# Edge counts as logarithms in the scores of graph layer 1, and softmax sums from a column of ones in its products

## The chip, the cores and the metric

The kernel runs on one core of a Trainium2 chip. The metric is the time of one execution on the device in microseconds (us). A profiled execution is looked at beside it: its span is the time from the first to the last instruction that the profiler saw.

## What is computed

Four graph networks work one after the other on 512 nodes with 768 features each, over 8704 edges; after each there is a residual addition and a normalisation. Layer 0 is a graph attention with eight heads, layer 1 a relational graph attention, layer 2 three relational convolutions, layer 3 two convolutions. The change is in layer 1, which has three edge types and is computed twice: with four heads of 192 features, then with one head of 768. One such convolution is:

```python
xr = jnp.einsum('nd,rdf->rnf', x, W)
oi, oj = xr[etype, dst], xr[etype, src]
alpha = leaky_relu(oi @ q + oj @ k, 0.2)
m = segment_max(alpha, dst)
e = exp(alpha - m[dst])
z = segment_sum(e, dst)
a = e / (z[dst] + 1e-16)
out = segment_sum(a * oj, dst)     # by heads; then the bias
```

Edges are not walked one by one. The kernel has counted how many edges of type r go from node n to node d, and keeps these counts c[d, r, n]. Then out[d] is the sum over (r, n) of c * exp(alpha - m) * xr[r, n], divided by the sum over (r, n) of c * exp(alpha - m).

## The kernel before, in words

Nodes lie in NB = 4 blocks of 128 partitions, and the three types side by side in the free dimension, so a score tile `z` has 128 x 1536 elements. All weights are used in a split form: `split_piece` (L735) loads a third of a 768 x 384 half of a matrix (`raw`, SP's queue), makes three parts of it (L753 on ScalarE, L754 and L755 on VectorE), and stays one half ahead of its use. `product` (L785) multiplies with these parts; between its first twelve and its last six matmuls of a block ScalarE scales the PSUM bank (L802).

**The counts.** `decode3` (L1168) runs four times inside the products of layer 0's heads 2 and 3: it takes three 3-bit digits out of a packed integer (L1175), ScalarE casts each to bf16 (L1176), SP stores 384 KB (`c3_store`), and VectorE sums and checks the counts (L1179 to L1184).

**Layer 1, first convolution.** Three types times two halves of `product` fill `xr[r]`; `columns` and `keys` make the two halves of the scores. Then `run` (L1374) goes through 16 steps s = (block b, head h). Its order is written out by hand: `soft` of step s+2, then the transposes (`turn`) of step s+1, then the sum of step s; Tile then orders each engine's instructions by its own priorities. A step is:
- `soft` (L1349): ScalarE makes z = key + column in three instructions (L1352). `softmax` (L833) takes the leaky maximum (L837, VectorE), negates, adds the mask and takes the minimum in one instruction (L839), takes the exponential (L843, ScalarE), multiplies by the counts while summing (L845, VectorE) and takes the reciprocal (L849).
- `turn` (L1357): twelve 128 x 128 transposes of z on TensorE (L1363), and three copies from PSUM (L1366), which `evacuate` gives to ScalarE and VectorE in turn (L84, L86).
- `sum1` (L1406): twelve matmuls of 192 columns (L1415; each fp32 matmul is two instructions in the profile), then one VectorE instruction that multiplies by the reciprocal and adds the bias (L1419). With a block's last head comes an ELU (L1424 to L1426), and a step later its transposes and split (L767 to L777).

`load_cm` (L1341) loads a block's counts, 384 KB in bf16, into one of two buffers, and makes the mask from them (L1346). z and the transposed weights have two buffers each.

**Layer 1, second convolution.** `product` fills `xr` again; as each block is complete, two dot products of 768 elements on VectorE (`dots`, L1440) give the scores' columns. The last ones gate the keys (L1450 to L1453), since these overwrite the rows that `dots` reads. Then `run` goes through four steps with 24 matmuls of 384 columns (L1473) in each.

Of the kernel before, what the change touches and what calls it, by code (L numbers as in the profile page):

```python
# [8 lines left out]
F32 = mybir.dt.float32  # L9
# [16 lines left out]
SOFT_EPS = 1e-16  # L26
LN_EPS = 1e-5
# [6 lines left out]
def gnn_stack_kernel(ctx: ExitStack, tc: tile.TileContext, a: dict, out: bass.AP):  # L34
# [73 lines left out]
    nc.vector.memset(eps, LN_EPS)  # L108
    ones = const.tile([P, 1], F32, tag="ones", name="ones")
# [46 lines left out]
    c3_store = dram.tile([NB, P, R3 * N], BF16, tag="c3", name="c3_store")  # L156
# [549 lines left out]
    def split_layers():  # L706
# [161 lines left out]
        with (  # L868
# [299 lines left out]
            def decode3(b):  # L1168

                v = work.tile([P, N], I32, tag="elu_y", name=f"packed_{b}")  # L1170
                nc.sync.dma_start(v, packed_store[b])
                c3 = g.tile([P, R3, N], BF16, tag="c3", name=f"c3_{b}")
                for r in range(R3):
                    d = work.tile([P, N], I32, tag="elu_e", name=f"d3_{b}_{r}")
                    digit(d, v, r)  # L1175
                    nc.scalar.copy(c3[:, r, :], d)  # L1176
                nc.sync.dma_start(c3_store[b], c3.rearrange("p r n -> p (r n)"))
                t = work.tile([P, N], F32, tag="elu_e", name=f"total_{b}")
                nc.vector.tensor_add(t, c3[:, 0, :], c3[:, 1, :])  # L1179
                nc.vector.tensor_tensor_reduce(  # L1180
                    out=t, in0=t, in1=c3[:, 2, :], scale=1.0, scalar=0.0,
                    op0=ALU.add, op1=ALU.add, accum_out=seen[:, 0, b : b + 1],
                )
                nc.vector.tensor_reduce(seen[:, 1, b : b + 1], t, axis=AX.X, op=ALU.max)  # L1184
# [88 lines left out]
        with (  # L1273
# [3 lines left out]
            xr = [rp.tile([P, NB, D], F32, tag=f"xr{r}", name=f"xr{r}") for r in range(R3)]  # L1277
# [9 lines left out]
            def columns(r, b):  # L1287

                rT = wide(f"r1_rT{r}_{b}")
                for j in range(2):  # L1290
                    pt = bank(f"r1_t{r}_{b}_{j}")
                    for i in range(HK):
                        c = j * HK + i
                        nc.tensor.transpose(
                            pt[:, i * P : (i + 1) * P], xr[r][:, b, c * P : (c + 1) * P], ident
                        )
# [26 lines left out]
            def project(left, r, j, name, also=None):  # L1323
                def keep(b, po):
                    evacuate(xr[r][:, b, columns_of(j)], po[:, :HD])
# [15 lines left out]
            def load_cm(b, name):  # L1341

                cnt = work.tile([P, R3 * N], BF16, tag="cnt", name=f"{name}_cnt{b}")
                nc.sync.dma_start(cnt, c3_store[b])
                mask = rp.tile([P, R3 * N], BF16, tag="mask", name=f"{name}_mask{b}")
                nc.vector.tensor_scalar(mask, cnt, 0.0, NEG, op0=ALU.is_equal, op1=ALU.mult)  # L1346
                return cnt, mask

            def soft(cm, key, bias, name):  # L1349
# [404 lines left out]
```

## Time and profile before

| | us |
|---|---|
| median of three runs | 1746.12 (1742.83 to 1746.43) |
| the profiled execution | 1745.2 |
| its span | 1743.3 |
| busy in the span: TensorE (PE) | 1614.6, 93% |
| VectorE (DVE) | 1219.2, 70% |
| ScalarE (ACT) | 755.7, 43% |
| layer 1's first run of 16 steps, from the first sum's first matmul to the last sum's end | 828.6 to 946.9 |

Times in rows are microseconds, those marked "mean ns" nanoseconds. PE is a matmul, PEld the load of its weights, SPq an issue of a transfer on SP's queue. A group's row gives the line, engine, operation, output and inputs with shapes, how often, then busy time and mean duration, then the idle time of the engine just before such instructions and what ended it. PEclk is the granted TensorE clock, 1.00 being full. One execution's 1.9 us outside its span are no part of the rows.

### The profile page before, as it was taken

How to read it: one execution, taken by the hardware profiler on the slowest of the kernel's cores; microseconds unless marked ns; L12 is line 12 of the kernel's file. 1: busy time of each engine (PE TensorE's matmuls, PEld its weight loads, DVE VectorE, ACT ScalarE, POOL GpSimd, SP SyncE). 2: the span in 40 equal slices, each digit the busy share in tenths (PEclk: the TensorE clock that was granted, in tenths of full speed). 3: DMA queues.
4: the chain of work that ended last, by engine and by line, in shares of the span. 5: the costliest groups of instructions: out<-in, count | busy, mean ns of one | idle time of the engine just before them, and what ended most of it. 6: DMA issues, size and time to landing. Idle time of an engine off the chain costs nothing.

```text
span 1743.3 us, 22110 instructions
## 1 busy us (share of the span) xinstructions
PE 1614.6 (93%) x8527; PEld 1446.1 (83%) x8527; DVE 1219.2 (70%) x2177; ACT 755.7 (43%) x1307; POOL 54.6 (3%) x62
## 2 busy tenths in 40 slices
PE   5999999999999996997878969999999999999897
PEld 2867979788797873996878966699999999999897
DVE  8977889686876877446995785466665547554764
ACT  5755555555555542334653433143334233423242
POOL 0000000000000002000001000000000001000001
PEclk9999999999999997998898989999999999999999
DMA  3323323231221321211001220243332324332321
GB/s 119 100 70 100 103 67 110 63 100 51 76 82 58 115 83 63 74 55 55 9 19 55 82 84 35 80 141 98 99 103 92 101 84 139 93 104 80 104 73 51
DMA packets 77699, 142.49 MB, mean 82 GB/s; under 512 B 5529, under 2 KB 65809, under 8 KB 75793
## 3 DMA queue, kind: packets, MB, share of 16 engines
q1 hardware_dynamic: 73264, 118.88, 22.1%
q0 software_dynamic: 3600, 20.47, 3.4%
q10 hardware_dynamic: 720, 1.64, 0.3%
q8 instruction: 69, 1.13, 0.3%
q14 instruction: 46, 0.37, 0.1%
HBM read 125.77 MB, written 15.20 MB: 81 GB/s over the span
## 4 chain that ended last, share of the span: by engine, by line
PE 85%; DVE 10%; ACT 3%; issue 1%; DMA 1%; ACTq 0%; DVEq 0%
PE g_o L1058 10%; PE c_p L807 6%; PE c_p L799 6%; PE c_p L796 6%; PE c_a L1514 4%; PE c_a L1518 4%; PE g_s L796 4%; PE g_s L799 4%; PE g_s L807 4%; PE r_o L1473 4%; PE g_p L796 3%; PE g_p L799 3%; PE g_p L807 3%; PE r_p L796 3%; PE r_p L799 3%; PE r_p L807 3%
## 5 line engine op out<-in xcount | busy, mean ns | idle before, releaser
L754 DVE SCALAR_TENSOR_TENSOR w<-w,raw 128x768 fp32r<-128x768 f32 x234 | 222.2, 956 | 120.9 <-ACT w L753 118.1
L753 ACT ACTIVATE w<-raw 128x768 fp32r<-128x768 f32 x234 | 194.8, 839 | 127.6 <-PE c_p L796 32.8
L755 DVE TENSOR_TENSOR w<-w,w 128x768 fp32r<-128x768 f32 x234 | 219.2, 952 | 2.0 <-PE g_p L807 1.0
L799 PE MATMUL c_p<-w,s 128*128 128x384 f32 x576 | 192.5, 334 | 0.0
L796 PE MATMUL c_p<-w,s 128*128 128x384 f32 x576 | 192.5, 334 | 0.0
L1058 PE MATMUL g_o<-wT,g_h 128*128 128x512 f32 x384 | 166.8, 594 | 5.8 <-ACT wT L1014 5.8
L1058 PEld LDWEIGHTS g_o<-wT,g_h 128*128 128x128 f32 x384 | 72.3, 190 | 95.5 <-issue 86.3
L1502 DVE TENSOR_TENSOR c_h_lo<-c_p,c_h_hi 128x384 fp32r<-128x384 f32 x96 | 53.2, 554 | 129.8 <-ACT c_h_hi L1501 129.8
L796 PE MATMUL g_p<-w,s 128*128 128x384 f32 x384 | 134.1, 349 | 0.0
L1514 PE MATMUL c_a<-c_h_hi,c_cT 128*128 128x384 f32 (+1 forms) x384 | 131.1, 341 | 0.0
L796 PE MATMUL g_s<-w,y 128*128 128x384 f32 x384 | 130.5, 340 | 0.1
L1518 PE MATMUL c_a<-c_h_lo,c_cT 128*128 128x384 f32 x384 | 130.1, 339 | 0.0
L799 PE MATMUL g_p<-w,s 128*128 128x384 f32 x384 | 129.4, 337 | 0.1
L802 ACT ACTIVATE c_p<-c_p 128x384 f32<-128x384 f32 x96 | 45.6, 475 | 192.7 <-PE c_p L799 192.3
L799 PE MATMUL g_s<-w,y 128*128 128x384 f32 x384 | 128.7, 336 | 0.0
L807 PE MATMUL c_p<-w,s 128*128 128x384 f32 x576 | 117.8, 339 | 0.2 <-ACT c_p L802 0.2
L796 PEld LDWEIGHTS c_p<-w,s 128*128 128x128 f32 x576 | 108.2, 188 | 0.0
L799 PEld LDWEIGHTS c_p<-w,s 128*128 128x128 f32 x576 | 108.1, 188 | 0.0
L807 PEld LDWEIGHTS c_p<-w,s 128*128 128x128 f32 x576 | 100.1, 188 | 5.5 <-ACT c_p L802 5.5
L796 PE MATMUL r_p<-w,s 128*128 128x384 f32 x288 | 100.0, 347 | 0.0
L799 PE MATMUL r_p<-w,s 128*128 128x384 f32 x288 | 98.8, 343 | 0.0
L1363 PE MATMUL soft_wt<-ident,r_z 128*128 128x128 f32 x240 | 39.9, 333 | 47.8 <-DVE r_den L845 47.8
(255 smaller groups left out, 3346.1 us busy)
## 6 DMA issues: line engine op xcount, KB each, us to landing
raw<-in_L_gnn_W_dram SPq DMA_DIRECT2D x216, 384.0 KB
c_cT<-cT_store POOLq DMA_DIRECT2D x8, 1024.0 KB, 5.7
raw<-in_L_gnn_root_dram SPq DMA_DIRECT2D x18, 384.0 KB
cT_store<-c_cT SPq DMA_DIRECT2D x4, 1024.0 KB
g_s<-in_L_gnn_a_src_dram POOLq DMA_DIRECT2D x8, 384.0 KB, 4.1
g_d<-in_L_gnn_a_dst_dram POOLq DMA_DIRECT2D x8, 384.0 KB, 4.5
r_cnt<-c_store SPq DMA_DIRECT2D x8, 384.0 KB
acc<-x_store SPq DMA_DIRECT2D x8, 384.0 KB
```

The source lines that it names most:

```text
L753: nc.scalar.mul(hm, w, ROUND / SPLIT)
L754: nc.vector.scalar_tensor_tensor(lo, hm, -SPLIT, w, op0=ALU.mult, op1=ALU.add)
L755: nc.vector.tensor_sub(df, hm, lo)
L796: nc.tensor.matmul(po[:, :HD], left[0][:, k, bs], hm[:, k, :], start=(k == 0), stop=False)
L799: nc.tensor.matmul(po[:, :HD], left[1][:, k, bs], lo[:, k, :], start=False, stop=(k == KC - 1))
L802: nc.scalar.mul(po[:, :HD], po[:, :HD], SPLIT + 1.0)
L807: nc.tensor.matmul(po[:, :HD], left[2][:, k, bs], df[:, k, :], start=False, stop=(k == KC - 1), skip_group_check=True,)
L1058: nc.tensor.matmul(po, self.h[k][:, c * P : (c + 1) * P], wT[:, k, :], start=(k == 0), stop=(k == NB - 1),)
L1473: nc.tensor.matmul(po[:, :HD], wT[:, k, :], source(k, columns_of(j)), start=(k == 0), stop=(k == NK - 1),)
L1502: nc.vector.tensor_sub(lo, po[:, :HD], hi)
L1514: nc.tensor.matmul(po[:, : HD + ones], cT[:, k, bs], h[0][:, k, : HD + ones], start=(k == 0), stop=False,)
L1518: nc.tensor.matmul(po[:, :HD], cT[:, k, bs], h[1][:, k, :], start=False, stop=(k == NB - 1))
```

## The change

- `decode3` no longer stores counts. ScalarE takes the logarithm of each digit plus 2^-60, VectorE pushes negative ones (no edge) to about -4e31, and SP stores each type by itself: three stores of 256 KB in fp32 for one of 384 KB in bf16. The tile of logarithms has one buffer.
- `load_cm` becomes `load_log`: 768 KB in fp32 a block, into one buffer, and no mask is made. `soft` adds the logarithm where the mask was added; the multiplication by the counts is gone.
- `xr` gets columns of ones (offsets 0, 385 and 770 of 772), so the data begin one or two elements later. Each first-convolution product has 193 columns, the second's first half 385. The extra column of the result is the softmax sum; `share` makes the reciprocal after the product.
- `turn` gives two of three copies to ScalarE and the third to VectorE.
- `dots` works on halves: four dot products of 384 elements and an addition for each block and type.

```diff
-                c3 = g.tile([P, R3, N], BF16, tag="c3", name=f"c3_{b}")
+                d = []
                 for r in range(R3):
-                    d = work.tile([P, N], I32, tag="elu_e", name=f"d3_{b}_{r}")
-                    digit(d, v, r)
-                    nc.scalar.copy(c3[:, r, :], d)
-                nc.sync.dma_start(c3_store[b], c3.rearrange("p r n -> p (r n)"))
-                t = work.tile([P, N], F32, tag="elu_e", name=f"total_{b}")
-                nc.vector.tensor_add(t, c3[:, 0, :], c3[:, 1, :])
+                    d.append(work.tile([P, N], I32, tag="elu_e", name=f"d3_{b}_{r}"))
+                    digit(d[r], v, r)
+                    t = g.tile([P, N], F32, tag="log3", name=f"log3_{b}_{r}")
+                    nc.scalar.activation(t, d[r], AF.Ln, bias=tiny)
+
+                    nc.vector.scalar_tensor_tensor(t, t, -NEG, t, op0=ALU.mult, op1=ALU.min)
+                    nc.sync.dma_start(log3_store[b, :, r, :], t)
+                    if r == 1:
+                        total = work.tile([P, N], F32, tag="elu_y", name=f"total_{b}")
+                        nc.vector.tensor_add(total, d[0], d[1])
...
-            xr = [rp.tile([P, NB, D], F32, tag=f"xr{r}", name=f"xr{r}") for r in range(R3)]
+            xr = [rp.tile([P, NB, D + 4], F32, tag=f"xr{r}", name=f"xr{r}") for r in range(R3)]
+            for r in range(R3):
+                for c in (0, HD + 1, D + 2):
+                    nc.gpsimd.memset(xr[r][:, :, c : c + 1], 1.0)
+
+            def row_slice(lo, hi):
+
+                by = 1 + lo // HD
+                return slice(lo + by, hi + by)
...
-                cnt = work.tile([P, R3 * N], BF16, tag="cnt", name=f"{name}_cnt{b}")
-                nc.sync.dma_start(cnt, c3_store[b])
-                mask = rp.tile([P, R3 * N], BF16, tag="mask", name=f"{name}_mask{b}")
-                nc.vector.tensor_scalar(mask, cnt, 0.0, NEG, op0=ALU.is_equal, op1=ALU.mult)
-                return cnt, mask
+                t = rp.tile([P, R3 * N], F32, tag="log", name=f"{name}_log{b}")
+                nc.sync.dma_start(t, log3_store[b].rearrange("p r n -> p (r n)"))
+                return t
...
-                return z, softmax(z, cm[1], cm[0], name, False)
+                nc.vector.scalar_tensor_tensor(z, z, SLOPE, z, op0=ALU.mult, op1=ALU.max)
+                nmax = small.tile([P, 1], F32, tag="nmax", name=f"{name}_nmax")
+                nc.vector.tensor_tensor_reduce(
+                    out=z, in0=z, in1=log, scale=-1.0, scalar=BIG,
+                    op0=ALU.add, op1=ALU.min, accum_out=nmax,
+                )
+                nc.scalar.activation(z, z, AF.Exp, bias=nmax, scale=-1.0)
+                return z
+
+            def share(total, name):
+
+                den = small.tile([P, 1], F32, tag="den", name=f"{name}_den")
+                nc.vector.tensor_scalar_add(den, total, SOFT_EPS)
+                nc.vector.reciprocal(den, den)
+                return den
...
-                    evacuate(
-                        t[:, q * NB : (q + 1) * NB, :], pt.rearrange("p (k n) -> p k n", n=P)
-                    )
+                    copy = nc.scalar.copy if q < R3 - 1 else nc.vector.tensor_copy
+                    copy(t[:, q * NB : (q + 1) * NB, :], pt.rearrange("p (k n) -> p k n", n=P))
...
+                at = row_slice(h * HC, (h + 1) * HC)
+                odd = h % 2
+                at = slice(at.start - 1 + odd, at.stop + odd)
                 for k in range(NK):
                     nc.tensor.matmul(
-                        po[:, :HC], wT[:, k, :], source(k, cs), start=(k == 0), stop=(k == NK - 1)
+                        po[:, : HC + 1], wT[:, k, :], source(k, at),
+                        start=(k == 0), stop=(k == NK - 1),
                     )
                 y = rows[b]
+                den = share(po[:, HC * odd : HC * odd + 1], f"r1_{b}_{h}")
...
             def dots(r, b):
                 for s in range(2):
-                    junk = rp.tile([P, D], F32, tag="elu", name=f"r2_j{r}_{b}_{s}")
-                    dot(cols2[:, s, r, b : b + 1], xr[r][:, b, :], qk2[s], junk)
+                    for j in range(2):
+                        js = row_slice(j * HD, (j + 1) * HD)
+                        junk = rp.tile([P, D], F32, tag="elu", name=f"r2_j{r}_{b}_{s}_{j}")
+                        dot(
+                            parts2[:, j, s, r, b : b + 1], xr[r][:, b, js],
+                            qk2[s][:, columns_of(j)], junk[:, :HD],
+                        )
+                nc.vector.tensor_add(
+                    cols2[:, :, r, b], parts2[:, 0, :, r, b], parts2[:, 1, :, r, b]
+                )
```

## The prediction

> **What bounds the kernel now.** I read the page's slices first. TensorE is at 90% or more nearly everywhere, so an edit off TensorE pays only where TensorE waits. The dips after the middle are layer 1: slices 19 to 22 (784 to 959 us) have PE 7, 8, 7, 8 and the clock below full.
>
> ```profile
> PE   5999999999999996997878969999999999999897
> DVE  8977889686876877446995785466665547554764
> PEclk9999999999999997998898989999999999999999
> ```
>
> Then the busy times by stretch, cut at the first run's start-up, its 16 steps, the second convolution's products and its start-up.
>
> ```profile
> core 0: us, PE busy (x) PEld busy (x) DVE busy (x) ACT busy (x) POOL busy (x), PEclk, DMA share, GB/s
> 812.20:828.60 16.40, 4.96 (x27) 4.75 (x26) 13.44 (x17) 9.06 (x12) 0.00 (x0) 0.58 0.01 1
> 828.60:946.90 118.30, 94.45 (x572) 91.51 (x570) 101.41 (x140) 65.31 (x88) 1.08 (x2) 0.90 0.08 24
> 950.30:1028.00 77.70, 77.66 (x441) 77.31 (x442) 56.30 (x87) 30.42 (x56) 3.66 (x2) 0.98 0.27 83
> 1028.00:1052.60 24.60, 7.24 (x36) 6.12 (x35) 23.04 (x33) 11.27 (x16) 0.00 (x0) 0.60 0.27 80
> ```
>
> In the steps VectorE is busy 86%, the fullest engine, and TensorE works at clock 0.90. TensorE's waits in 812 to 947 have one large entry (us in total, times, longest), the multiplication by the counts, and the groups of the 16 steps give prices:
>
> ```profile
> PE soft_wt L1363 <- DVE r_den L845: 35.3, 10, 11.4
> ```
>
> ```profile
> L1415 PE MATMUL r_o<-xr,soft_wT 128*128 128x192 f32 x384 | 68.7, 338 | 0.0
> L1363 PE MATMUL soft_wt<-ident,r_z 128*128 128x128 f32 x170 | 26.8, 319 | 23.8 <-DVE r_den L845 23.8
> L1352 ACT ACTIVATE r_z<-r_kk,r_cols 128x512 f32<-128x512 f32 x40 | 26.4, 716 | 0.3 <-PE soft_wt L1363 0.3
> L845 DVE CUSTOM_DVE_ANT_0 r_z<-r_z,r_cnt 128x1536 f32<-128x1536 f32 x14 | 24.6, 1755 | 6.3 <-ACT r_z L843 6.2
> L843 ACT ACTIVATE r_z<-r_z,r_nmax 128x1536 f32<-128x1536 f32 x14 | 22.0, 1573 | 6.1 <-DVE r_nmax L839 5.9
> ```
>
> So VectorE bounds the steps: three instructions of 1.75 us, and the last stands between exponential and transposes.
>
> **The 16 steps: engine totals.** VectorE loses 14 x 1.84 = 25.8 (L845 with its 0.085 read of the sum), the masks (2.2), and 22 - 15 = 7 copies of 0.686 (4.8); it gains 16 additions on one PSUM column, each about the 0.17 us of the 128x8 copy at L1307: 2.7. 101.4 - 30.1 = 71. ScalarE gains 7 copies of 0.581: 65.3 + 4.1 = 69. TensorE keeps its work; 193 columns for 192 is 0.5%. Warm, twelve transposes take 1.31 us from start to start and 24 matmuls 3.90 (in the timeline 865.66, 866.97, and 48 of them in 7.97 less a tail); the cold transposes at 858.72 took 2.68. Floor: 16 x 3.90 + 15 x 1.31 + 3 x 0.65 (the x1b transposes) = 84.1. TensorE becomes the bound.
>
> **The cycle that follows.** The built order on each engine keeps TensorE at transposes(s+1), sum(s). With T the end of sum(s-1): transposes until T+1.36; only then is a z buffer free, and ScalarE makes z(s+3) in three steps, T+1.8 to T+3.75 (from start to start 0.65 each); the exponential of the next z ends at T+5.3; its transposes may start at T+5.5, which is when sum(s) ends (T + 1.36 + 3.90 = T+5.26, a little waiting for copies). VectorE in that time: the new sum's addition right after sum(s-1), the minimum by T+2.1, the reciprocal, the third copy by T+2.9, bias by T+3.3, the next leaky maximum by T+5.5. The addition waits for a sum on TensorE, and behind it in VectorE's queue stand minimum and third copy; both have over a microsecond left. So 5.35 us a step against 118.3 / 16 = 7.39 now: 16 x 5.35 = 85.6. To it come 2 for x1b, about 2 until the pipeline runs, and the ELU: 1.7 us on ScalarE ahead of copies, plus 1.0 of splits, with only about 0.2 us to spare in its loop; I take 2.4 for each of three blocks, 7. Sum 97; gain 21.3. Bounds: 88 (no ELU loss) and 107 (rival B).
>
> **The log load.** One buffer: the next block's load starts after the last minimum of the block, at T'+2.1, and the next minimum wants it at about T'+5.8, and can slip to T'+7.3 before the exponential is late. No row has 768 KB on SP's queue. The nearest: 384 KB issued at 1044.49 were there at 1047.65.
>
> ```profile
> 1044.49 5.76 SPq L1344 DMA_DIRECT2D r_cnt<-c_store  x2
> ...
> 1047.65 0.56 DVE L1346 TENSOR_SCALAR r_mask<-r_cnt 128x1536 bf16<-128x1536 bf16 x1 [0.84 <-DMA r_cnt<-c_store]
> ```
>
> 3.16 us: if size cost nothing it stays that, if all were size it is 6.3. The Trainium skill (DMA: Bandwidth & Descriptors, Anatomy of one DMA) divides a transfer into about 2.0 us fixed and bytes over 436 GB/s: 3.8 for 768 KB, and 2.9 for the 384 KB that took 3.16. Row plus the page's extra 0.9 is 4.1, my estimate. At 4.1 the slack hides the load and the single buffer costs 0; at 6.3 it costs about 1 at each of three blocks. I take 0. SP holds nothing urgent behind it.
>
> **Start-up of the first run.** No L845 between exponential and transposes: -1.75.
>
> **The second convolution.** Its products now have 24 x 2 half dots of 0.554 + 0.085 and 12 additions of 0.1 for 24 of 0.957 + 0.085: +0.6 for each of 12 blocks and types. Within the stretch VectorE has 56 of 78 us busy and the split weights arrive 2.5 to 3 us before use, which hides it. Not at the end: the last dots gate the keys. From 1020.8 on I lay the built order out: three blocks' extra 0.6 and the two weight instructions of 0.95 that now stand before them bring the last dot from 1034.1 to 1037.4, +3.3. Then L845 is missing before the first transposes (-1.75); but the second block's minimum waits for a log load issued only after the first's minimum (4.1 us, uncovered here), and its exponential stands behind z of block 2: the first sum starts at 1055.3 instead of 1052.6. +2.7, bounds +0.5 and +5. After that 48 matmuls a step hide everything; the first half's extra column is 0.1%.
>
> **decode3, four times in layer 0.** VectorE gets three instructions of 0.69 more: 8.3 in all; casts become logarithms of 0.1 more. Each head lasted 74.0 us with or without decode3 in the windows, so the old one was hidden. New are waits: the single log tile makes ScalarE's next logarithm wait for the last store. Here is the nearest wait, ScalarE held until 384 KB were stored, 2.76 us after issue:
>
> ```profile
> 188.12 0.32 SPq L1177 DMA_DIRECT2D c_store<-c  x1
> ...
> 190.88 0.62 ACT L1176 CAST c<-d 128x512 bf16<-128x512 int32 x1 [1.11 <-DMA c_store<-c]
> ```
>
> Behind it in ScalarE's queue stand the scaling L802 (a block of TensorE work, about 1.4 us spare) and weight pieces (about 6 us ahead); behind VectorE's wait the dots and the next head's softmax, whose last z was ready at 229.1 for transposes at 231.8: 2.7 spare. Work of 4.2 for each of two heads plus waits of some 3, less the 3.4 idle that VectorE had there, overruns this by about 1.
>
> Logarithm and exponential need different tables: four more loads. The Trainium skill speaks against that (ScalarE: Activation LUTs, What ACT_TABLE_LOAD costs): 1.28 plus a 1.38 drain, 2.66 a switch. The row here is 1.28 (819.08), and the exponential started at 820.38, with no drain to be seen. By the page ScalarE loses 10.6, by the row 5.1; I take the row, and both lie beside a ScalarE that is busy 41 of 74. Together +3; bounds 0 (all in the idle time) and +28 (rival C).
>
> **At nothing:** the nine memsets of ones on GpSimd's queue ahead of the loads of q and k. By its row of 1.82 us for a far larger tile they take at most 16; q and k were loaded at 706 and first used at 728.4. An offset of 4 or 8 bytes in `xr`: no row shows it for fp32; no gain is possible; I take 0.
>
> **Sum:** -21.3 - 1.75 + 2.7 + 3 = -17.3. Span 1743.3 - 17.3 = 1726.0; with the 1.9 around it 1727.9; the median lies 0.9 above the profiled execution: 1728.8, so **1729**.
>
> **Rivals.**
> - A, as above: 1729, with 1718 (no ELU loss, decode3 hidden) to 1736. 0.62.
> - B, ScalarE's loop takes VectorE's place. z, exponential, copies and ELU are 69 of 97 us in strict order, with two z buffers and 0.2 us spare. If each hand-over costs some 0.2 more, a step is 6.2: 99 + 2 + 6 = 107, the gain shrinks to 11.3 and the time is 1739. For it: hand-overs of 0.2 between engines everywhere. Against: z can be made in part before the exponential. 0.26.
> - C, slower. Place: decode3's waits for its stores, ten of them. Each can hold L802 for the whole 2.8 us; were none covered, 28 us of TensorE would be lost in layer 0, against 20 won: 1754. It decides from about 2.0 us lost a wait. For it: SP issues weight loads behind these stores too. Against: the row above waited 1.1 of its 2.8, and TensorE lost nothing. 0.07.
> - D, the edit doesn't free VectorE: each addition stops its queue until a sum ends, a wait in place of L845. Were it stopped 2.8 us a step, most of a sum of 3.9, VectorE's 71 would become 71 + 16 x 2.8 = 116, a gain of 2 + 1.75 - 2.7 - 3: 1748. Against: at the addition, TensorE is just through with that sum in the order laid out above. 0.05.
>
> **How the numbers follow.** A and most of B lie within 1716 to 1743. A measurement of this kernel can tell about 0.2% (3.5 us) from no change, so "same" is 1742.6 to 1749.6: D and B's end, 0.06. Slower: C, 0.07. Faster: 0.87.
>
> **What would show it.** Right: TensorE's clock near 1.0 in the steps, some 95 to 100 us from first to last sum, no group of VectorE releasing the transposes but ScalarE's exponential; the last half dot about 3 us later against the products' end; TensorE's idle time in heads 2 and 3 unchanged. Wrong: PE waiting for L802 or weights in heads 2 and 3 (C), transposes waiting over 1 us a step for the exponential (B), minima that wait for a log load, or sums slower than 3.9 us.

## The result, and the profile after

The changed kernel takes 1730.2 us (median of four runs, 1729.5 to 1732.6), against 1745.6 for the kernel before on the same chip (1742.8 to 1746.4). The ratio is 0.9917 (95% interval 0.9900 to 0.9934): 0.8% faster, 1.2 us above the forecast of 1729. The profiled execution took 1729.9, its span is 1727.1; before it was 1743.3, so the spans differ by 16.2.

The three rows of the changed kernel's slices that answer to those of before:

```profile
PE   5999999999999995999788959999999999999897
DVE  8977888796868778554784874565666546654764
PEclk9999999999999997999799989999999999999999
```

The dips of TensorE are fewer and shorter, and in layer 1's first run (slices 20 to 22, 820 to 950 us) the clock's digit is below 9 in the first slice only. The stretches of the changed kernel, cut as before (columns: the stretch, its length, then busy time of each engine, granted clock, DMA):

```profile
core 0: us, PE busy (x) PEld busy (x) DVE busy (x) ACT busy (x) POOL busy (x), PEclk, DMA share, GB/s
819.58:835.30 15.72, 6.24 (x28) 5.84 (x29) 9.71 (x11) 9.89 (x13) 0.00 (x0) 0.50 0.00 1
835.30:932.80 97.50, 87.83 (x572) 85.84 (x570) 73.56 (x117) 67.77 (x95) 1.08 (x2) 0.96 0.14 45
936.90:1014.00 77.10, 77.06 (x437) 76.75 (x436) 60.15 (x139) 30.07 (x56) 3.86 (x2) 0.98 0.27 83
1014.00:1039.60 25.60, 7.52 (x37) 6.36 (x37) 18.15 (x31) 12.99 (x19) 0.00 (x0) 0.61 0.34 108
```

The 16 steps last 97.5 us instead of 118.3, VectorE is busy 75% of them instead of 86%, and TensorE's clock is 0.96 instead of 0.90. TensorE's waits from 819 to 935 us now name other releasers (us in total, times, longest):

```profile
PE soft_wt L1395 <- ACT r_z L1379: 13.9, 4, 9.2
PE x1b_t L770 <- DVE r_den L1386: 4.3, 2, 2.1
```

The transposes (`soft_wt`) wait for ScalarE's exponential. 9.2 of the 13.9 us is the start-up; within the steps 4.7 are left, where VectorE's multiplication had caused 23.8. New are 5.0 us for the ELU's transposes (`x1b_t`), 4.3 of them in the second row. The groups of the 16 steps that answer to those of before:

```profile
L1449 PE MATMUL r_o<-xr,soft_wT 128*128 128x193 f32 x384 | 67.3, 334 | 0.0
...
L1370 ACT ACTIVATE r_z<-r_kk,r_cols 128x512 f32<-128x512 f32 x39 | 26.2, 722 | 0.3 <-PE soft_wt L1395 0.3
L1375 DVE CUSTOM_DVE_ANT_0 r_z<-r_z,r_log 128x1536 f32<-128x1536 f32 x14 | 24.6, 1757 | 0.8 <-DMA r_log<-log_store 0.8
...
L1395 PE MATMUL soft_wt<-ident,r_z 128*128 128x128 f32 x170 | 22.0, 280 | 4.7 <-ACT r_z L1379 4.7
L1379 ACT ACTIVATE r_z<-r_z,r_nmax 128x1536 f32<-128x1536 f32 x14 | 22.0, 1573 | 5.5 <-DVE r_nmax L1375 3.6 <-DVE r_den L1385 1.9
```

Only the mean of the transposes has changed by more than 3%, 280 ns for 319; their durations in the timeline go with the clock (twelve of them take 1.47 us warm, 2.68 in the cold case of the kernel before). The steady state is short enough to be read from TensorE's own timeline: start, duration, group.

```profile
853.61 1.47 PE L1395 MATMUL soft_wt<-ident,r_z 128*128 128x128 f32 x12
854.92 4.09 PE L1449 MATMUL r_o<-xr,soft_wT 128*128 128x193 f32 x24
858.84 1.47 PE L1395 MATMUL soft_wt<-ident,r_z 128*128 128x128 f32 x12
...
867.69 0.84 PE L770 MATMUL x1b_t<-ident,r_y 128*128 128x128 f32 x6 [2.14 <-DVE r_den L1386]
```

From transposes to transposes it is 5.23 us (853.61 to 858.84), with no gap; the sum of 193 columns takes as long as that of 192 did (4.09 and 4.07). There are fourteen such intervals between the sums' starts, and the last two sums take 8.0: 81.2 us without any wait. The other 16.2 are 3.9 in the first two intervals (a wait of 2.0 and a cold clock), 2.0 for the transposes of three blocks (`x1b`), and 10.3 lost at and behind the ELU of these blocks: five waits of 7.7 in all, the rest mostly a cold clock behind the last of them.

Where the 16.2 us of span came from and went, from the profiled executions of both kernels (differences are taken before rounding):

| stretch | before | after | difference | predicted |
|---|---|---|---|---|
| to the first head's sums | 98.0 | 98.3 | +0.3 | 0 |
| layer 0, from there to the last head's sums | 505.9 | 513.2 | +7.3 | +3 |
| from there to the first run's first sum | 224.7 | 223.9 | -0.9 | -1.75 |
| the 16 steps | 118.2 | 97.5 | -20.8 | -21.3 |
| second convolution, to its first sum | 105.7 | 106.8 | +1.2 | +2.7 |
| its sums, to layer 2 | 71.1 | 70.5 | -0.6 | 0 |
| layers 2 and 3 | 619.6 | 617.0 | -2.7 | 0 |

So the total came closer to the forecast than the single terms did: layer 0 lost 4.3 more than said, and 2.7 that no term of the sum contains came back at the start of layer 2. That is luck.

### The profile page after: what moved, and what is told of

Its sections match the earlier page's. It is cut to its first block, busy times and chain, and to the rows that moved or that the text cites. A ratio compares the mean times of both kernels' runs of the same rounds, so it can differ in the third digit from the quotient of the medians.

```text
span 1727.1 us, 22203 instructions
## 1 busy us (share of the span) xinstructions
PE 1614.3 (93%) x8527; PEld 1443.7 (84%) x8527; DVE 1187.5 (69%) x2212; ACT 767.8 (44%) x1321; POOL 54.2 (3%) x71
## 4 chain that ended last, share of the span: by engine, by line
PE 82%; DVE 9%; ACT 4%; DMA 2%; issue 1%; ACTq 0%; DVEq 0%
PE g_o L1061 10%; PE c_p L810 6%; PE c_p L802 6%; PE c_p L799 6%; PE c_a L1565 4%; PE c_a L1569 4%; PE g_s L799 4%; PE g_s L802 4%; PE r_o L1522 4%; PE g_s L810 3%; PE r_p L799 3%; PE r_p L802 3%; PE r_p L810 3%; PE g_p L799 3%; PE g_p L802 3%; PE g_p L810 2%
## 5 line engine op out<-in xcount | busy, mean ns | idle before, releaser
L799 PE MATMUL g_p<-w,s 128*128 128x384 f32 x384 | 134.7, 351 | 0.0
L802 PE MATMUL g_p<-w,s 128*128 128x384 f32 x384 | 129.7, 338 | 0.1
L810 PE MATMUL c_p<-w,s 128*128 128x384 f32 x576 | 117.9, 339 | 0.0
L810 PEld LDWEIGHTS c_p<-w,s 128*128 128x128 f32 x576 | 100.0, 188 | 5.3 <-ACT c_p L805 5.3
L810 PE MATMUL g_p<-w,s 128*128 128x384 f32 x384 | 79.4, 340 | 1.5 <-ACT g_p L805 1.4
```

The costliest lines, as they stand in the source:

```text
L799: nc.tensor.matmul(po[:, :HD], left[0][:, k, bs], hm[:, k, :], start=(k == 0), stop=False)
L802: nc.tensor.matmul(po[:, :HD], left[1][:, k, bs], lo[:, k, :], start=False, stop=(k == KC - 1))
L810: nc.tensor.matmul(po[:, :HD], left[2][:, k, bs], df[:, k, :], start=False, stop=(k == KC - 1), skip_group_check=True,)
```

## Experiments

Each kernel is the changed one with one edit, unless said otherwise; times stand beside runs of the kernel before on the same chip, as ratios with their 95% intervals. Differences of one or two us are read in their own stretch of the profile, since the runs of one kernel spread by 2 to 8 us.

### Why every head of layer 0 is slower

Heads 2 and 3 contain `decode3`, the others do not. Yet in the changed kernel heads 5 to 7 lasted 74.4 us each instead of 73.9, without a wait of TensorE that was not there before. Only one of the two products was slower. These are the groups of the second matmul of a pair from 380 to 620 us, before and after; the number behind the busy time is the mean ns:

```profile
L799 PE MATMUL g_s<-w,y 128*128 128x384 f32 x144 | 48.4, 336 | 0.0
L799 PE MATMUL g_p<-w,s 128*128 128x384 f32 x144 | 48.1, 334 | 0.0
```

```profile
L802 PE MATMUL g_s<-w,y 128*128 128x384 f32 x152 | 51.5, 339 | 0.0
L802 PE MATMUL g_p<-w,s 128*128 128x384 f32 x144 | 48.1, 334 | 0.0
```

The durations overlap, so the distance between starts says more: 0.1734 us in `g_s` before, 0.1767 after. `g_p` and layer 2's products did not change. `g_s` alone reads the tile Y, which lies at the far end of the memory. The new constant `tiny` takes a slot of 32 bytes near its beginning and pushes up what is laid out behind it, weights, S and z among them, but not Y: in the built programs the first weights start at byte 55584 of a partition before the change and at 55616 after it, Y at 192480 in both. Three runs tested that, and a fourth bears on it.

**The constant without a slot.**

```diff
-    eps = const.tile([P, 1], F32, tag="eps", name="eps")
+    small_values = const.tile([P, 2], F32, tag="eps", name="eps")
+    eps, tiny = small_values[:, 0:1], small_values[:, 1:2]
...
-    tiny = const.tile([P, 1], F32, tag="tiny", name="tiny")
```

> The constant 2^-60 is a second column of the tile of the other small constant, so that it takes no slot of its own and every tile behind it lies 32 bytes lower, where it lay before the change; nothing else differs. Theory P (placement): layer 0's heads are 0.47 us slower even without decode3 because the new slot moved the weights, but not the tile Y at the other end of the memory, so the product that reads both has its matmuls 0.177 us apart where 0.173 were. Then heads 4 to 7 last 73.9 us again instead of 74.4, and eight heads give 3.5 to 3.9 us: a profiled span of 1723.4, a time about 3.6 below the changed kernel's 1730.2. Theory Q (left-over load: the decode3 work shifts queues of ScalarE and VectorE against TensorE for the rest of the layer): nothing moves, the span stays within 1 of 1727.1 and heads 4 to 7 last 74.4.

Head 4 lasted 74.25, as before the change, heads 5 to 7 lasted 73.92; starts in `g_s` 0.1734 apart. 1728.9 us, ratio 0.9901 (0.9887 to 0.9914), span 1724.5. The stretch of layer 0 gave 2.3 us, less than the 3.5 expected, because `decode3`'s part happened to be 0.7 larger. The heads' durations are those of theory P.

**The kernel before with the slot alone.**

```diff
+    tiny = const.tile([P, 1], F32, tag="tiny", name="tiny")
+    nc.vector.memset(tiny, 2.0**-60)
```

> The kernel before the change with nothing but an unused constant of one column in a slot of its own, so that the weights, S and z lie 32 bytes higher and Y where it was. Theory P: layer 0's product with Y slows from 0.1734 to 0.1767 us a matmul, heads 4 to 7 last 74.4 us instead of 73.9, and the time is 3.5 to 3.8 us above the kernel before (0.2%). Rival (the loss comes from the changed work or from the other tiles' new places): heads of 73.9 us, no difference in time.

Heads 5 to 7 lasted 74.4 us, and the groups, same stretch as above, show the slower `g_s` of the changed kernel:

```profile
L801 PE MATMUL g_s<-w,y 128*128 128x384 f32 x147 | 49.8, 339 | 0.0
L801 PE MATMUL g_p<-w,s 128*128 128x384 f32 x144 | 48.1, 334 | 0.0
```

1749.3 us against 1746.0, ratio 1.0023 (1.0015 to 1.0031). An unused tile of four bytes a partition costs 0.2%: the effect is one of placement and has nothing to do with the work that the change does.

**Y moved as well.**

```diff
+            gap = ypools.enter_context(tc.tile_pool(name="g_gap", bufs=1, side="right"))
+            nc.gpsimd.memset(gap.tile([P, 8], F32, tag="gap", name="gap"), 0.0)
             ypool = ypools.enter_context(tc.tile_pool(name="g_y", bufs=1, side="right"))
```

> The changed kernel with the tile Y moved by 32 bytes as well (a 32-byte tile is put before it), so that Y and the weights lie to each other as before the change, while the weights themselves stay 32 bytes higher. If the distance between the two operands counts, the result is that of the run without the extra slot: heads of 73.9 us, 3.5 to 3.9 us gained. If the weights' own address counts, heads stay at 74.4 us and nothing is gained. By theory Q nothing is gained either.

Heads 5 to 7 at 74.3, starts in `g_s` 0.1760 apart; 1733.2 us, ratio 0.9930 (0.9913 to 0.9947). But the edit did not do what it was meant to. Tiles of the right side are laid out from the end of the memory downwards, so the new tile moved Y down, to byte 192448, away from where it would have restored the distance. From the first weights to Y it is 136896 bytes before the change, 136864 after it, and 136832 here. The expectation about the distance was therefore not tested; the run only adds a third placement, and a slow one.

A fourth placement is that of the run with load on VectorE below: four more slots of 32 bytes put the weights at byte 55744, 128 above those of the changed kernel, with Y at 192480. There heads 5 to 7 lasted 73.97 with starts 0.1735 apart. So neither a higher address of the weights nor a shorter distance to Y slows the product as such. Whether the distance counts or the addresses themselves, and which are slow, stays open.

### What decode3 costs

Beyond the placement, heads 2 and 3 lose 2.5 and 1.5 us in the changed kernel (76.91 and 75.91 against 74.39). Over the nine profiles with the same `decode3` the sum of both is 3.7 to 4.9. TensorE's waits of the changed kernel in these two heads:

```profile
PE g_o L1061 <- ACT wT L1017: 3.0, 3, 1.4
PE g_k L866 <- DVE g_cols L858: 1.6, 2, 1.2
PE g_p L810 <- ACT g_p L805: 1.1, 2, 0.8
PE g_s L810 <- ACT g_s L805: 0.5, 1, 0.5
```

The first was there before (three waits, 2.9 us); the others are new, 3.2 us: the next head's keys wait for dots that are late on VectorE, and the last six matmuls of a block wait for ScalarE's scaling, which stands behind a logarithm. ScalarE's own wait for the stores, and its timeline, show what held that:

```profile
ACT log L1181 <- DMA log_store<-log: 10.0, 6, 2.1
```

```profile
186.35 1.28 ACT L1181 ACT_TABLE_LOAD   x1
187.65 0.72 ACT L1181 ACTIVATE log<-d,tiny 128x512 f32<-128x512 int32 x1
...
204.70 0.72 ACT L1181 ACTIVATE log<-d,tiny 128x512 f32<-128x512 int32 x1 [1.72 <-DMA log_store<-log]
205.33 0.47 ACT L805 ACTIVATE g_p<-g_p 128x384 f32<-128x384 f32 x1
```

The logarithm at 204.70 waits 1.72 us for the store of the tile before it, and the scaling stands behind it. The table load is 1.28 us, and the logarithm at 187.65 follows at once.

**Three buffers.**

```diff
+            lpool = ypools.enter_context(tc.tile_pool(name="g_log", bufs=3, side="right"))
...
-                    t = g.tile([P, N], F32, tag="log3", name=f"log3_{b}_{r}")
+                    t = lpool.tile([P, N], F32, tag="log3", name=f"log3_{b}_{r}")
```

> The changed kernel with three buffers for the logarithms that layer 0 stores, in free memory beside Y; the slot of the constant stays. Heads 2 and 3 now last 76.91 and 75.91 us, 2.52 and 1.52 more than heads 5 to 7 (74.39). Theory S (the stores): ScalarE waits 4.4 and 5.6 us there for the store of the tile before it, and these waits pass on to TensorE; with three buffers they vanish, heads 2 and 3 come within 1 us of 74.4, and 2 to 4 us are gained. Theory V (the work itself: 4.2 us more on VectorE a head, logarithms and table loads on ScalarE): the two heads keep at least 3 of their 4 us, and at most 1 is gained.

ScalarE's 10.0 us of waiting for stores vanish from the list. Heads 2 and 3 last 75.20 and 75.75, 0.8 and 1.4 above the later ones: 2.2 of the 4.0 remain, so neither theory holds alone. 1732.1 us (0.9911, 0.9891 to 0.9930): no gain in the time. In the profiled execution 2.1 us more than in that of the changed kernel went ahead of the first head's sums, and 2.6 more between layer 0's last head and the first run, with the same instructions: 1.3 in the last attention of layer 0 and 1.4 on a colder clock at the end of the first convolution's columns (below).

**And without the push.** Beside the three buffers, the instruction that takes negative logarithms down to -4e31 is left out.

```diff
...
-                    nc.vector.scalar_tensor_tensor(t, t, -NEG, t, op0=ALU.mult, op1=ALU.min)
```

> The changed kernel with three buffers for the stored logarithms, and without the VectorE instruction that pushes negative ones to -4e31 (this part of the computation is left out: an absent edge then counts as 2^-60). With three buffers heads 2 and 3 kept 0.81 and 1.36 us over the later heads' 74.39. If VectorE's added work is what remained (2.1 us of these instructions in each half head pair, dots and so the next head's keys late behind them), the two heads now come within 0.4 us each of the later ones. If it is ScalarE's part (logarithms, table loads), they keep at least 1.5 us together.

Head 2 is at 74.44, 0.06 above the later heads: there VectorE's added work was the rest. Head 3 stays at 75.58. It loses elsewhere now: its keys no longer wait for the dots, but VectorE waits once 3.1 us for the load of the packed counts (1.6 with the push), and the head's first product takes 25.5 us, 24.3 with the push. That the one makes the other is argued, not shown. So for head 2 the expectation held, for head 3 it did not; what would remain of head 3 without that load was not tried. 1727.7 us, ratio 0.9896 (0.9879 to 0.9912).

### What freed the 16 steps: VectorE's load or the link

The multiplication by the counts was both work on the fullest engine and a link between exponential and transposes. Two kernels put back the work, one in the link and one beside it.

**In the link.**

```diff
                 nc.scalar.activation(z, z, AF.Exp, bias=nmax, scale=-1.0)
+                nc.vector.scalar_tensor_tensor(z, z, 1.0, z, op0=ALU.mult, op1=ALU.max)
                 return z
```

> One VectorE instruction of 1.75 us (the maximum of z and z, in place) is put back between the exponential and the transposes, 16 times in the first run and 4 times in the second; sums still come from the column of ones. Theory A (both VectorE's load and this link bounded the steps): VectorE's 73.6 us in the steps become 73.6 + 16 x 1.75 = 101.6, the steps last 112 to 118 us again instead of 97.5, the start-ups get 1.75 longer twice: 1746 to 1753, all of the gain or more is lost. If only VectorE's load counted and the place did not, it equals the next run. If the gain came from something else (two of three copies on ScalarE, no masks), the loss is below 8 us.

The instruction stands in `soft`, so it also runs four times in the second convolution. The stretch of the 16 steps, columns as above:

```profile
838.03:952.50 114.47, 94.77 (x572) 91.23 (x570) 96.69 (x131) 69.16 (x96) 1.08 (x2) 0.91 0.12 39
```

And what TensorE waited for from 822 to 955 us, the only row there:

```profile
PE soft_wt L1396 <- DVE r_z L1380: 31.0, 9, 11.4
```

The old picture is back, down to the clock of 0.91: 114.5 us. The time is 1751.5 against 1746.7 before, ratio 1.0032 (1.0019 to 1.0044). With this instruction back in its place the change is a loss. All else that the edit does in the steps (no masks, other copies, the sums from the column of ones) is left with the 3.8 us between 114.5 and the 118.3 before.

**Beside it.**

```diff
...
+                nc.vector.tensor_reduce(
+                    extra, kk[:, h].rearrange("p r n -> p (r n)"), axis=AX.X, op=ALU.max
+                )
...
```

> The same amount of VectorE work in each of the 16 steps, but off the path: a maximum over a key tile of 1536 elements into one column that nobody reads, some 1.6 us each. Theory A: VectorE gets 73.6 + 26 = 99.6 us of work, more than the 97.5 that the steps last, so the steps go to about 103 to 110 us and the time to 1736 to 1743: about half of the gain is lost. Rival (only the link between exponential and transposes had mattered): the steps stay within 3 us of 97.5 and the time within 3 us of 1730. Other rival (only VectorE's load had mattered): as much is lost as with the instruction in the link.

```profile
834.55:936.30 101.75, 88.28 (x571) 84.59 (x570) 91.90 (x129) 68.45 (x95) 1.08 (x2) 0.97 0.13 43
```

```profile
L1433 DVE TENSOR_REDUCE r_x<-r_kk 128x1 f32<-128x1536 f32 x12 | 20.8, 1739 | 0.0
```

18.3 us more of VectorE's time in this stretch (91.9 for 73.6) cost 4.3 us; in the link 23.1 more cost 17.0. Four of these sixteen instructions already ran ahead of the stretch, two of those in the link. Counted from the last key matmuls on, so that all sixteen are in (1.74 us each beside the link, 1.75 in it), it is 5.5 us against 18.5. The steps stayed below the range that theory A gave (103 to 110) and above that of the rival. VectorE is busy 90% of this stretch, more than the 86% before the change, and the steps are 16.5 us shorter than they were then. So a high load alone was not what had bounded them; in these profiles the place of the instruction was the larger part. (Six kernels whose edits don't touch the steps have 95.7 to 97.7 us there, so that differences below 2 us say little.)

The times make the two parts less unequal. This kernel takes 1738.7 us, ratio 0.9958 (0.9943 to 0.9972), within theory A's 1736 to 1743, and its profiled execution is the fastest of its five, 5.0 below the median. By the ratios it is 7 us slower than the changed kernel, although its layer 0 is 2.5 us shorter where its tiles happen to lie better (above); the kernel with the instruction in the link is 20 slower, some 2.5 of them in the second convolution. Set against each other like that it is about 10 us for the load and 17 or 18 for load and place together, each uncertain by some 4 us. Where a typical execution loses the rest no profile here shows.

**Copies in turn**, as before the change.

```diff
-                    copy = nc.scalar.copy if q < R3 - 1 else nc.vector.tensor_copy
-                    copy(t[:, q * NB : (q + 1) * NB, :], pt.rearrange("p (k n) -> p k n", n=P))
+                    evacuate(
+                        t[:, q * NB : (q + 1) * NB, :], pt.rearrange("p (k n) -> p k n", n=P)
+                    )
```

> The changed kernel with the copies of the transposes given to ScalarE and VectorE in turn, as before the change, instead of two of three to ScalarE. By theory A TensorE paces the steps at 5.23 us each and VectorE has room: it gets 7 copies more (4.8 us, 73.6 to 78.4 of 97.5), ScalarE 7 fewer; the steps stay between 96 and 100 us and the time within 3 of 1730. Rival: VectorE is again too full where its three instructions of a step meet the copy, and the split of two to one carries part of the gain: the steps go above 101 us.

The steps last 99.3, 1.8 more; VectorE has 77.6 us of work in them. 1731.6 us (0.9919, 0.9902 to 0.9937). The expectation of theory A held; the split of two to one is worth no more than these 1.8, which lie within the 2 us that say little.

**The ELU's transposes one step later.**

```diff
-                if h == 1 and b:
+                if h == 2 and b:
                     finish1(b - 1)
```

> The changed kernel with the transposes of a finished block put one step later: after the transposes of the third head's weights instead of the second's. Nothing else moves. In the steps TensorE waits 2.14, 0.72 and 2.14 us for the ELU there, with a cold clock after the last (sum of 5.13 instead of 4.09, transposes of 1.51 for 0.85). Theory E (the ELU pinch is this wait on TensorE): the steps go from 97.5 to 90 to 93.5 us, the time down by 4 to 7. Rival (the pinch is the ELU's work on ScalarE and VectorE, which makes the exponentials behind it late, 1.07 and 1.59 us behind block 2): the steps stay within 2 us of 97.5.

```profile
836.70:930.40 93.70, 86.84 (x571) 84.37 (x570) 73.21 (x117) 67.81 (x95) 1.08 (x2) 0.98 0.14 47
```

3.7 us less, just outside the range for theory E, and 1.6 of these come in the first two intervals, ahead of any ELU, where the clock was warm sooner. So 2.1 are the edit's. Within the steps TensorE waits for the exponential alone:

```profile
PE soft_wt L1395 <- ACT r_z L1379: 6.7, 6, 2.2
```

The 5.0 us of waiting for the ELU are gone, but the waits for the exponential behind the start rise from 2.7 to 5.2: half of what was taken from one wait came back as another. Ahead of the longest one (895.27) two ELU instructions stand on ScalarE between the score instructions, and one of 0.96 us on VectorE, which fits the rival. Both theories hold in part. 1727.1 us, ratio 0.9889 (0.9871 to 0.9907).

### The start of the second convolution

Times here count from the start of the products' last six matmuls (L807 before, L810 after), since the clock also moves what lies ahead. The first leaky maximum follows them by 10.4 us in the kernel before and by 12.3 in the changed one, the first sum by 25.9 and 26.6.

**A second place for the logarithms.**

```diff
+            def load_log2(b):
+                if b % 2 == 0:
+                    return load_log(b, "r2")
+                t = kk2[:, 1].rearrange("p r n -> p (r n)")
+                nc.sync.dma_start(t, log3_store[b].rearrange("p r n -> p (r n)"))
+                return t
...
```

> The changed kernel; in the second convolution the logarithms of blocks 1 and 3 are loaded into a free quarter of the key tile, so that block 1's need not wait for block 0's minimum. The built order then also has block 1's exponential ahead of block 2's scores on ScalarE. Theory L (the one buffer counts here, where nothing covers the load): the wait of 3.01 us ahead of block 1's minimum goes, its exponential ends at about 1034.0 instead of 1037.0, and the first sum comes 2.5 to 3 us earlier: 103.8 to 104.3 us after the end of the first run's sums, for 106.8. Rival (the last dots alone set the start): within 0.5 of 106.8.

VectorE's and ScalarE's lines for block 1, first in the changed kernel, then here:

```profile
1033.58 1.76 DVE L1375 CUSTOM_DVE_ANT_0 r_z<-r_z,r_log 128x1536 f32<-128x1536 f32 x1 [3.01 <-DMA r_log<-log_store]
...
1035.41 1.56 ACT L1379 ACTIVATE r_z<-r_z,r_nmax 128x1536 f32<-128x1536 f32 x1
```

```profile
1030.41 1.76 DVE L1375 CUSTOM_DVE_ANT_0 r_z<-r_z,r_kk 128x1536 f32<-128x1536 f32 x1
...
1032.55 1.57 ACT L1379 ACTIVATE r_z<-r_z,r_nmax 128x1536 f32<-128x1536 f32 x1 [0.38 <-DVE r_nmax L1375]
```

The first sum comes 24.0 us after those six matmuls: 2.6 gained, theory L. (From the first run's end it is 105.0, only 1.9 less, as the way to these matmuls took 0.8 longer.) 1729.8 us, 0.9909 (0.9891 to 0.9927).

**Whole dots.**

```diff
...
-                    for j in range(2):
-                        js = row_slice(j * HD, (j + 1) * HD)
-                        junk = rp.tile([P, D], F32, tag="elu", name=f"r2_j{r}_{b}_{s}_{j}")
-                        dot(
-                            parts2[:, j, s, r, b : b + 1], xr[r][:, b, js],
-                            qk2[s][:, columns_of(j)], junk[:, :HD],
-                        )
+                    junk = rp.tile([P, D + 1], F32, tag="elu2", name=f"r2_j{r}_{b}_{s}")
+                    dot(cols2[:, s, r, b : b + 1], xr[r][:, b, 1 : D + 2], qk2[s], junk)
```

> The changed kernel with whole dots again: each dot runs over 769 elements with the column of ones in the middle, against a row that holds a zero there; two dots of about 1.04 us each for four of 0.64 and an addition. Theory D (the split dots delay the start of the second convolution): some 0.6 us a block less on VectorE, which is full between the products' end and the keys, so the first keys' maximum comes 2.2 us nearer to the products' end, where it was before the change, and the first sum 1.5 to 2.5 us earlier: 104.3 to 105.3 after the first run's sums. Rival (VectorE is not the bound there, weight pieces and copies are): within 0.5 of 106.8.

From the six matmuls to the first maximum 10.5 us, to the first sum 24.9: 1.8 gained each, theory D. From the first run's end it is 106.3, only 0.5 less, since the way to these matmuls took 1.3 longer. 1728.8 us, 0.9902 (0.9884 to 0.9919).

### Together

> Five edits of the changed kernel together: the constant without a slot of its own, three buffers for the stored logarithms, the transposes of a finished block one step later, the second convolution's loads into a free quarter of the key tile, whole dots. If they add up, the sum of what each gave in its own stretch is 3.7 + 1.9 + 3.7 + 2.6 + 1.8 = 13.7 us: heads 4 to 7 at 73.9, heads 2 and 3 at about 75, steps of 93 to 94 us, the first sum of the second convolution 22 to 23 us behind the products' last six matmuls (26.6 now), and 1716 to 1720 in all, which would be the fastest here. If whole dots and the second log place hide each other, as much as 2 less.

1722.7 us (1721.3 to 1723.5) against 1746.0, ratio 0.9872 (0.9856 to 0.9888): the fastest kernel here, and its interval lies below the changed kernel's, though the 1716 to 1720 expected were missed. Layer 0 gave 4.8 (heads 2 and 3 at 75.0 and 74.9, heads 5 to 7 at 73.9), the steps 3.7 (of which again 1.6 at their start), and the first sum comes 22.2 us after the six matmuls, 4.5 earlier: near what was expected, 13.0 of 13.7. Yet the span fell by 7.6: the columns ahead of the first run took 1.5 longer, the second convolution up to the six matmuls 1.0, and all from its first sum to the end 2.6. The instructions there are the same. At the columns the granted clock was 0.77 over the last 21.9 us (0.89 over as much in the changed kernel), and the transposes ahead of layer 2 were cold (1.51 us for 0.84); that the clock took all of the 5.1 us was not shown.

## Why the prediction was right, and where it was not

- **The 16 steps: right in the mechanism, and in the sum partly by luck.** 97.5 for 97, intervals of 5.23 us for 5.35, VectorE 73.6 us for 71, ScalarE 67.8 for 69, a clock of 0.96. The cycle as laid out, transposes until T+1.3 and a sum of 3.9, is what the timeline shows. But three terms were off and cancel. The steps were put at 16 x 5.35 = 85.6 and took 81.2: besides the shorter interval, the transposes of two of the sixteen steps lie ahead of the stretch. The ELU was put at 7 and cost 10.3, or 3.4 for each of three blocks instead of 2.4, the one late log load included. Until the pipeline ran, 2 was said and 3.9 came.
- **"VectorE bounds the steps" was only part of the reason.** The instruction costs 5.5 us beside the path and 18.5 in it by the profiles, about 10 and 17 or 18 by the times. It was the last of the three, at its place, that had to go; the engine's total alone would have promised as much for any other instruction of that length.
- **Start-up of the first run: 1.3 instead of 1.75.** From the last four key matmuls (819.83) to the first sum it is 15.5 instead of 16.8. The twenty-four transposes there took 5.32 us instead of 4.90, with a mean clock of 0.50 instead of 0.58 in this stretch; that is the missing 0.4.
- **The log load: estimate too small, conclusion right where it counted.** The loads took 4.4 to 4.7 us in the second convolution and 5.3 at one block boundary, where 4.1 was the estimate from the row and the Trainium skill (DMA: Bandwidth & Descriptors, Anatomy of one DMA). The page's own 3.8 is further off; that section gives it for transfers that GpSimd issues, and these are on SP's queue. At the block boundaries one minimum waited, 0.8 us, instead of none. Uncovered, one buffer costs 2.6.
- **Second convolution: +2.7 said, +0.7 measured from the products' end, +1.2 with the products.** The failed term is the last dots: +3.3 was laid out, 1.9 measured, and undoing the halves gave back 1.8. Three blocks of 0.6 account for all of it; the two weight pieces that were said to come ahead in addition did not delay the last dot further. The other term, from maximum to first sum, was -0.6 in the forecast and is -1.2.
- **decode3: +3 said, 4.0 measured, within 0 to 28.** The chain is the one named: store waits on ScalarE, work on VectorE, then the next head's dots. Ten waits of up to 2.8 were feared; six of at most 2.1 came. Removing the store waits gives about half. The sign "TensorE's idle time in heads 2 and 3 unchanged" failed, with 3.2 us of new waits; 1.6 of them are for the scaling, the sign of rival C in a small size. The choice between the skill's page (ScalarE: Activation LUTs, What ACT_TABLE_LOAD costs), 2.66 a switch, and the row, 1.28, is settled for the row: from the load's start to that of the logarithm it is 1.30 us (186.35 to 187.65), with no room for a drain.
- **Missing: the placement.** The forecast had no term for the constant that the change adds, and it costs 0.47 us in each of eight heads, 3.7 (3.3 of it in the row of layer 0 above). "Nothing" was said of memsets and of the shifted columns of `xr`, and no wait or longer sum shows that they cost anything; the tile that was overlooked moved the rest of the memory.
- **Missing: the clock ahead of and at the start of layer 2**, which gave back 2.8 in the profiled execution. The error of +4.3 in layer 0 and this one cancel in large part, which is luck; without that clock the execution would have taken about 1733, 4 above the forecast.
- **Rivals.** B (a ScalarE loop of 6.2 us) did not come: 5.23, and it is TensorE that has no gap. C (waits of over 2 us lost on TensorE) did not come. D did not: VectorE waits for sums 8.0 us in the steps, in three places.

## What to carry to other kernels

A busy engine and a late link look the same in the shares; the same instruction put back beside the path and in the path tells them apart. Here about half (by the times) to two thirds (by the profiles) of its cost belonged to its place in the path. Count tiles as well as instructions: a new constant moves what lies behind it, and the pace of a matmul can depend on that by 2%. When an edit moves a tile, look up where it went: one here moved it the wrong way. And read a difference of some us in its own stretch of the profile: clock phases elsewhere give or take as much.

## What the runs showed of the hardware

**Placement.** Shifting the weights by 32 bytes, with the other operand in its place, moved the distance between matmuls of 384 columns from 0.1734 to 0.1767 us in one product and in none of the others, with no wait recorded; 128 bytes further it was 0.1735.

**The clock after a short pause follows a fixed grid.** Ahead of layer 2 TensorE waits 2.8 to 2.9 us for a normalisation in each of the fourteen profiles. In seven the six transposes behind it take 0.84 to 0.88 us, in the other seven 1.46 to 1.54, followed by up to fourteen weight-product matmuls 0.32 us apart instead of 0.17. First before the change, then after:

```profile
1122.49 1.54 PE L767 MATMUL x_t<-ident,r_y 128*128 128x128 f32 x6 [2.79 <-DVE r_y L831]
```

```profile
1109.51 0.84 PE L770 MATMUL x_t<-ident,r_y 128*128 128x128 f32 x6 [2.88 <-DVE r_y L834]
```

From the transposes to the first group of six matmuls of the product it is 7.7 us before and 4.9 after, the 2.8 that no part of the change explains.

Which of the two comes can be read from the traces. In each profile all changes of the granted clock lie a multiple of 3.413 us apart, and where this grid begins differs from profile to profile. Here are the two steps of the grid at this pause, before the change (the clock, third from the end, falls to 0.50) and after (it does not):

```profile
1118.33:1121.74 3.41, 1.37 (x5) 0.49 (x3) 1.58 (x5) 0.29 (x1) 0.55 (x1) 1.00 0.25 53
1121.74:1125.15 3.41, 2.66 (x11) 2.66 (x12) 1.80 (x4) 0.98 (x2) 0.00 (x0) 0.50 0.97 372
```

```profile
1104.95:1108.36 3.41, 1.68 (x6) 0.66 (x4) 1.42 (x4) 0.20 (x1) 0.55 (x1) 1.00 0.21 24
1108.36:1111.77 3.41, 2.26 (x15) 2.29 (x16) 2.02 (x5) 0.97 (x3) 0.00 (x0) 1.00 0.93 370
```

In the first TensorE had been idle for 60% of the step when the clock fell, in the second for 51%. Over the fourteen profiles the longest idle share of such a step at this pause is 60 to 84% in the seven cold ones and 46 to 57% in the seven warm ones. So the same pause costs up to 2.8 us or nothing, by where it falls on the grid, which no edit here was made to set. The Trainium skill (TensorE: Matmul & The Clock Gate, Part 1: The HAM clock gate) has the clock set by a window of 3.4 us that runs freely, which agrees with the grid; but it names a whole idle window as the condition, and here 60% of one sufficed.

The clock also falls without a pause of over 0.3 us where TensorE does small work: at the end of the first convolution's columns the clock over the last 21 to 22 us was 0.89 in the changed kernel's profile and 0.72 in that with three log buffers, 1.4 us in time, though the instructions there are the same.
